# Two activations an octet in place of one over both layers, with the bias moved from TensorE into the activation, in a graph message kernel on one core

## The chip, the cores and the metric

One core of a Trainium2 chip. The metric is the device time of one execution in microseconds (us), the median of three runs, lower is better. The engines are named as in the profile: PE (TensorE matmuls), PEld (its weight loads), DVE (VectorE), ACT (ScalarE), POOL (GpSimd) and SP (SyncE, which here only issues DMAs).

## What is computed

```
x: 12500 x 64, src, dst: 400000 edges (dst sorted), edge_attr: 400000 x 16
m_in     = concat(x[src], x[dst], edge_attr)              # 144 wide
h        = silu(m_in @ W1 + b1)                           # 64 wide
messages = silu(h @ W2 + b2)
agg      = segment_sum(messages, dst)
out      = layernorm(x + silu(concat(x, agg) @ W3 + b3))
```

All of it is float32.

## The kernel before

The edges are cut into 3125 tiles of 128 edges, and eight tiles make an **octet**, so there are 391 octets; three octets make a chunk, for which destinations and attributes are loaded together. Because dst is sorted, an octet's edges fall in a window of 48 nodes. The first layer is split by its inputs. x W1a is a table in DRAM (`pa`), of which rows are gathered by source node. x W1b of the octet's 48 nodes, and W1c below it, stand in the weights `xw`, which multiply a one-hot matrix `oh` that has the attributes below it. Through the first 60 octets x W1b is computed by octet (`window_product`, `window_copy`); meanwhile `table_b` writes it for all nodes to a zero-padded DRAM table `pw1b`, 256 nodes at a time in octet steps 8 to 56, and from octet 60 (`OWN`) on SP fetches an octet's 48 rows from that table. In the kernel before, both ways add b1 on PE, by a matmul of a row of ones with `b1r` (lines 413 and 440).

The messages of an octet are summed on PE into `pg` by a second one-hot matrix `eh` (`add_up`, line 538), and DVE adds that to the window of the resident sums `agg` (`add_window`, line 543).

The source rows come in three ways. POOL gathers most with indirect DMAs of 128 rows (line 390). A tile pair of some octets (`pairs`) instead takes columns of the resident x, `xs`, copied one by one into a tile `cx` by ACT (`nc.scalar.copy`, line 317) and DVE (`tensor_reduce` over one element, line 315), with the column's address in a register that is loaded eight at a time (line 298), and PE multiplies them by W1a. A pair is 256 columns, so that every 256/144 = 1.78 octets one pair, two gathers, is taken from POOL. `ACOLS` and `VCOLS` say how many columns an octet step has on ACT and on DVE, each in two parts. A few pairs (`rpairs`) are fetched by SP row by row, 16 rows a step (line 341). The addresses of the columns are loaded by SP (line 368) into three rotating tiles `cxi` and scaled by DVE (line 376).

PE, ACT, DVE and SP run in the order written in the loop over octets, `for o in range(NO + 1)`. Within step o of the kernel before each engine has, in order:

- SP: index loads, `load` for the chunk that begins at o + 2, `window_load(o + 3)`, 16 rows.
- DVE: `add_window(o - 4)`, `compare_dst(o + 1)`, 40 columns, `window_copy(o + 1)` while o + 1 is below 60, `compare_nodes(o + 1)`, 32 columns, then addresses and node work.
- PE: `window_product(o + 1)`, `first_layer(o)`, `second_layer(o - 1)`, `table_b`, `add_up(o - 2)`, and in some steps a node product (lines 570 to 573).
- ACT: 72 columns, one Silu over 1024 elements a partition (line 524: the first layer of octet o and the second of o - 1, which share a two-bank PSUM tile `p12` and an output tile `hm`), the copy of `table_b`'s product (line 415) and its DMA to `pw1b` (line 416), and in some steps a node Silu (line 579).

Engines meet through semaphores. DMAs of SP and ACT share eight semaphores in rotation, and each of them waits until the DMA that had its semaphore before has completed.

Of the kernel before, what the change touches and what calls it, by code (L numbers as in the profile page):

```python
# [9 lines left out]
F32 = mybir.dt.float32  # L10
# [3 lines left out]
AF = mybir.ActivationFunctionType  # L14
OP = mybir.AluOpType
AX = mybir.AxisListType
PSUM = bass.MemoryType.PSUM
DRAM = bass.MemoryType.DRAM
ENG = mybir.EngineType

P = 128
G = 4
CT = 24
OT = 8
# [5 lines left out]
OWN = 60  # L30
XWB = 5
TABLES = 7
ACOLS = (40, 32)
VCOLS = (40, 32)
ROWS = 16
LOADS = 8
XBASE = (0, 64 << 18)
XADDR = 37344
LAG = CT * P // 32

U = 125
# [60 lines left out]
def windows(ctx, tc, ident, badi, pa, pw1b, x, xt, src_c, src_row, dst_c, dst_row, attr_t, dst_2, attr_2, base, w1, b1, w2, b2, w3, b3, out, edges):  # L102
    nc = tc.nc
    N, D = x.shape
# [3 lines left out]
    NO = base.shape[1]  # L108
    assert 2 * (S + A) == P and N + S <= NP
    E = 2 * S  # L110
    const = ctx.enter_context(tc.tile_pool(name="fconst", bufs=1))
# [16 lines left out]
    w1ab = const.tile([D, 2, D], F32, name="w1ab")  # L128
# [4 lines left out]
    nc.scalar.dma_start(left, b2.rearrange("(o k) -> o k", o=1))  # L133
    w1d = const.tile([P, P], F32, name="w1d")
    nc.vector.memset(w1d, 0.0)
    b1r = const.tile([1, 2, D], F32, name="b1r")
    nc.scalar.dma_start(b1r, b1.rearrange("(o s k) -> o s k", o=1, s=1).to_broadcast([1, 2, D]))
    w2d = const.tile([P, P], F32, name="w2d")
    nc.vector.memset(w2d, 0.0)
    w3s = const.tile([P, D], F32, name="w3s")  # L140
    for s in range(2):
        h = slice(s * D, (s + 1) * D)
        nc.scalar.dma_start(w1d[h, h], w1[0:D, :])
    XC = 2048
    xs = fast.tile([P, NP], F32, name="xs")

# [105 lines left out]
    octs = []  # L252
# [4 lines left out]
    with tc.tile_pool(name="gat", bufs=AHEAD + 2) as gat, tc.tile_pool(name="drp", bufs=2) as drp, \  # L257
            tc.tile_pool(name="hot", bufs=2) as hot, \
            tc.tile_pool(name="ehp", bufs=5) as ehp, \
            tc.tile_pool(name="work", bufs=2) as work, tc.tile_pool(name="win", bufs=3) as win, \  # L260
            tc.tile_pool(name="ps1", bufs=2, space=PSUM) as ps1, \
            tc.tile_pool(name="psa", bufs=1, space=PSUM) as psa, \
            tc.tile_pool(name="cx", bufs=4) as cx, tc.tile_pool(name="cxi", bufs=3) as cxi, \
            tc.tile_pool(name="rx", bufs=2) as rx, tc.tile_pool(name="rxi", bufs=2) as rxi, \
# [38 lines left out]
        def columns(o, eng, part):  # L303
            for j, e0, n in pieces(o, eng, part):
                regs = addresses(eng, j, e0, n)
                if pairs[j] not in cols:
                    cols[pairs[j]] = cx.tile([P, P], F32, name="cx")
                t = cols[pairs[j]].bitcast(U8)
                s = e0 // P
                h = slice(s * D, (s + 1) * D)  # L310
                for e, r in zip(range(e0 % P, e0 % P + n), regs):
                    to, frm = t[h, 4 * e:4 * e + 4], xb[h, ds(r - (XBASE[s] + XADDR), 4)]
                    if eng == ENG.DVE:

                        nc.vector.tensor_reduce(to, frm[:, :, None], AX.X, OP.max)  # L315
                    else:
                        nc.scalar.copy(to, frm)  # L317
# [53 lines left out]
        def address(o):  # L371
            for j in begun(o):
                t = indices[j]
                for s in range(2):
                    h = slice(s * P, (s + 1) * P)
                    nc.vector.tensor_scalar(t[:, h], t[:, h], 4.0, float(XBASE[s] + XADDR), op0=OP.mult, op1=OP.add)  # L376

# [26 lines left out]
        def table_b(c):  # L404

            n = min(2 * P, NP - c)
            k = (n + P - 1) // P
            ps = mis.tile([P, 2, D], F32, name="mm")
            t = pbs[c // (2 * P) % 2]
            for i in range(k):  # L410
                p = min(P, n - i * P)
                nc.tensor.matmul(ps[:p, i, :], xs[0:D, c + i * P:c + i * P + p], w1ab[:, 1, :], start=True, stop=False)
                nc.tensor.matmul(ps[:p, i, :], ones[:, :p], b1r[:, 0, :], start=False, stop=True)
            if n == 2 * P:
                nc.scalar.copy(t[:, :, D:], ps)
                nc.scalar.dma_start(pw1b[c:c + n, :].rearrange("(i p) d -> p i d", p=P), t)
                return
            for i in range(k):
                p = min(P, n - i * P)
                nc.scalar.copy(t[:p, i, D:], ps[:p, i, :])  # L420
                nc.scalar.dma_start(pw1b[c + i * P:c + i * P + p, :], t[:p, i, :])
# [14 lines left out]
        def window_product(o):  # L436
            pw = mis.tile([P, P], F32, name="mm")
            nc.tensor.matmul(pw[:E, :], winrow[o].rearrange("k s w -> k (s w)"), w1bb.rearrange("k s m -> k (s m)"),
                             start=True, stop=False)
            nc.tensor.matmul(pw[:E, :], ones[:, :E], b1r.rearrange("o s k -> o (s k)"), start=False, stop=True)  # L440
            winrow[o] = pw

        def window_copy(o):
# [10 lines left out]
                nc.sync.dma_start(dr[k * S:(k + 1) * S, e], dst_2[1 - k:2 - k, d].to_broadcast([S, e.stop - e.start]))  # L454
            nc.sync.dma_start(oh[E:, e], attr_2[:, d])

        hots, both, outs, messages, nodes_of = {}, {}, {}, {}, {}

        def compare_dst(o):
            c, t0, n, first, last = octs[o]  # L460
# [15 lines left out]
        def first_layer(o):  # L476
            c, t0, n, first, last = octs[o]
            n2 = n + n % 2
            k = n2 // 2
            ga = got.pop(o)  # L480
            oh, eh = hots.pop(o)
            both[o] = ps1.tile([P, 2, OT // 2, P], F32, name="p12")
            outs[o] = work.tile([P, 2, OT // 2, P], F32, name="hm")
            p1 = both[o][:, 0]
            nc.tensor.matmul(p1[:, :k], xw[o % XWB], oh, start=True, stop=False, skip_group_check=True)  # L485
            if o < RAW:
                pt = mis.tile([P, OT // 2, P], F32, name="mm")
                for i in range(k):
                    nc.tensor.matmul(pt[:, i, :], ga[:, 2 * i:2 * i + 2, :].rearrange("p s d -> p (s d)"), ident,
                                     start=True, stop=True)  # L490
                xg = outs[o][:, 0]
                nc.vector.tensor_copy(xg[:, :k], pt[:, :k])
                nc.tensor.matmul(p1[:, :k], w1d, xg[:, :k], start=False, stop=True, skip_group_check=True)
            if o in pairs:
                nc.tensor.matmul(p1[:, 0, :], w1d, cols.pop(o), start=False, stop=False, skip_group_check=True)  # L495
            for i in range(1 if o in pairs else 0, k if o >= RAW else 0):
                g2 = single.pop(o) if o in rpairs and i == 1 else ga[:, 2 * i:2 * i + 2, :]
                nc.tensor.matmul(p1[:, i, :], g2.rearrange("p s d -> p (s d)"), ident,  # L498
                                 start=False, stop=(i == k - 1), skip_group_check=True)
            nodes_of[o] = eh  # L500

        def second_layer(o):
            c, t0, n, first, last = octs[o]
            n2 = n + n % 2
            k = n2 // 2
            h = made.pop(o)
            if o + 1 == NO:
                both[NO] = ps1.tile([P, 2, OT // 2, P], F32, name="p12")
                outs[NO] = work.tile([P, 2, OT // 2, P], F32, name="hm")
            p2 = both[o + 1][:, 1].rearrange("p i (s d) -> p (i s) d", s=2)  # L510
            nc.tensor.matmul(p2[:, :n2, :], one3, b2r[:, :n2, :], start=True, stop=False, skip_group_check=True)  # L511
            for i in range(k):
                nc.tensor.matmul(p2[:, 2 * i:2 * i + 2, :].rearrange("p s d -> p (s d)"), h[:, i, :], w2d,  # L513
                                 start=False, stop=(i == k - 1), skip_group_check=True)

        def silus(o):

            pp = both.pop(o)
            hm = outs.pop(o)
            columns(o, ENG.Activation, 0)  # L520
            columns(o, ENG.Activation, 1)
            k = [-(-octs[q][2] // 2) if 0 <= q < NO else 0 for q in (o, o - 1)]
            if k == [OT // 2, OT // 2]:
                nc.scalar.activation(hm, pp, AF.Silu)  # L524
            else:
                for j in range(2):
                    if k[j]:
                        nc.scalar.activation(hm[:, j, :k[j]], pp[:, j, :k[j]], AF.Silu)
            made[o] = hm[:, 0]
            messages[o - 1] = hm[:, 1].rearrange("p i (s d) -> p (i s) d", s=2)  # L530

        def add_up(o):
            c, t0, n, first, last = octs[o]
            m, eh = messages.pop(o), nodes_of.pop(o)
            pg = sums[:, o % 4, :]
            for i in range(n):
                s = i % 2
                nc.tensor.matmul(pg[s * D:(s + 1) * D, :], m[:, i, :], eh[:, i, :],  # L538
                                 start=(i < 2), stop=(i >= n - 2), skip_group_check=True)
# [116 lines left out]
        with tc.manual_schedule(engines={ENG.PE, ENG.Activation, ENG.DVE, ENG.SP}):  # L656
            compare_dst(0)
            compare_nodes(0)
            for o in range(NO + 1):
# [59 lines left out]
                if o >= 1:  # L719
                    for c in tables[(o - 1) * per:o * per]:  # L720
                        table(c)
                if o >= 1:
                    second_layer(o - 1)
                silus(o)
                if 8 <= o < 8 + len(tables_b):
                    table_b(tables_b[o - 8])
                if o >= 2:
                    add_up(o - 2)
                address(o + 2)
                raddress(o + 2)  # L730
                rows(o)
# [295 lines left out]
```

## Time and profile before

| | us |
|---|---|
| median of 3 runs | 3783.2 |
| lowest, highest | 3776.93, 3786.62 |
| the profiled execution | 3786.62 |
| its span | 3784.8 |

| engine | busy us | share of the span |
|---|---|---|
| ACT | 3132.3 | 83% |
| DVE | 2711.0 | 72% |
| PE | 2674.0 | 71% |
| POOL | 2514.3 | 66% |

The profile is one execution, the highest of the three runs. Register loads, semaphore waits and DMA issues do not count as busy, so an engine that spends time on them can be full well below 100%. A group line gives an operation's line in the code, its engine, out<-in, shapes and count; then busy time and the mean length of one; then the idle time of the engine ahead of it and what ended that. "issue" means that nothing the profile shows ended it.

### The profile page before, as it was taken

How to read it: one execution, taken by the hardware profiler on the slowest of the kernel's cores; microseconds unless marked ns; L12 is line 12 of the kernel's file. 1: busy time of each engine (PE TensorE's matmuls, PEld its weight loads, DVE VectorE, ACT ScalarE, POOL GpSimd, SP SyncE). 2: the span in 40 equal slices, each digit the busy share in tenths (PEclk: the TensorE clock that was granted, in tenths of full speed). 3: DMA queues.
4: the chain of work that ended last, by engine and by line, in shares of the span. 5: the costliest groups of instructions: out<-in, count | busy, mean ns of one | idle time of the engine just before them, and what ended most of it. 6: DMA issues, size and time to landing. Idle time of an engine off the chain costs nothing. (4 is left out here: it accounts for less than half of the span.)

```text
span 3784.8 us, 115732 instructions
## 1 busy us (share of the span) xinstructions
PE 2674.0 (71%) x14985; PEld 1907.6 (50%) x14985; DVE 2711.0 (72%) x29094; ACT 3132.3 (83%) x27519; POOL 2514.3 (66%) x2666
## 2 busy tenths in 40 slices
PE   7988887766676676766666667666676666676666
PEld 5666565544454554544444444444454444454444
DVE  1376666777777777777777777777777777777775
ACT  2277777989889889898889898898898988988985
POOL 7665555667666667676676676676766666766763
PEclk9766667776767667777776767777667777666777
DMA  5532222223232232222323223223232232322322
GB/s 113 122 64 57 61 61 61 60 58 67 59 66 63 60 66 58 64 61 57 67 60 67 62 59 66 59 58 65 61 64 58 64 67 58 66 60 57 66 59 51
DMA packets 200383, 243.23 MB, mean 64 GB/s; under 512 B 86481, under 2 KB 139290, under 8 KB 198698
## 3 DMA queue, kind: packets, MB, share of 16 engines
q1 hardware_dynamic: 86360, 130.76, 15.0%
q0 software_dynamic: 85024, 87.23, 12.4%
q10 hardware_dynamic: 28210, 17.75, 1.9%
q14 instruction: 663, 5.43, 0.5%
q8 instruction: 126, 2.06, 0.2%
HBM read 222.64 MB, written 12.87 MB: 62 GB/s over the span
## 5 line engine op out<-in xcount | busy, mean ns | idle before, releaser
L390 POOL DMA_INDIRECT ga<-pa,sc x2561 | 2421.4, 945 | 1180.6 <-issue 672.7
L317 ACT COPY cx<-xs 64x4 uint8 x27016 | 2701.7, 188 | 169.0 <-issue 108.4
L315 DVE TENSOR_REDUCE cx<-xs 64x4 uint8 x27000 | 2062.7, 147 | 813.1 <-issue 764.8
L538 PE MATMUL pg<-eh,hm 128*64 128x48 f32 x6250 | 367.7, 280 | 899.1 <-DVE agg L543 898.7
L538 PEld LDWEIGHTS pg<-eh,hm 128*64 128x64 f32 x6250 | 309.2, 190 | 968.4 <-DVE agg L543 958.1
L485 PE MATMUL p<-oh,xw 128*128 128x512 f32 (+1 forms) x782 | 740.9, 1047 | 0.8 <-PE pg L538 0.5
L498 PEld LDWEIGHTS p<-ident,ga 128*128 128x128 f32 x2562 | 538.4, 296 | 153.2 <-issue 150.1
L513 PE MATMUL p<-w2d,hm 128*128 128x128 f32 x3126 | 519.9, 316 | 129.2 <-ACT hm L524 128.9
L513 PEld LDWEIGHTS p<-w2d,hm 128*128 128x128 f32 x3126 | 441.5, 218 | 259.6 <-ACT hm L524 150.8
L524 ACT ACTIVATE hm<-p 128x1024 f32<-128x1024 f32 x389 | 396.4, 1019 | 177.8 <-PE p L513 170.8
L498 PE MATMUL p<-ident,ga 128*128 128x128 f32 x2562 | 541.3, 377 | 0.0
L466 DVE TENSOR_TENSOR oh<-dr,wrow 96x512 f32<-96x512 int32 x391 | 263.0, 673 | 21.4 <-DMA dr<-in_dst 21.0
L495 PEld LDWEIGHTS p<-cx,w1d 128*128 128x128 f32 x422 | 135.2, 320 | 202.8 <-issue 202.8
L472 DVE TENSOR_TENSOR eh<-wrow,dc 128x384 f32<-128x384 f32 x391 | 213.9, 547 | 2.5
L485 PEld LDWEIGHTS p<-oh,xw 128*128 128x128 f32 x782 | 178.2, 283 | 39.9 <-issue 9.9
L511 PE MATMUL p<-b2r,one 3*128 3x512 bf16 x391 | 189.1, 484 | 0.0
L543 DVE TENSOR_TENSOR agg<-agg,pg 128x48 f32 x391 | 78.2, 200 | 130.2 <-PE pg L538 72.1
L579 ACT ACTIVATE z<-mm 128x256 f32<-128x256 f32 (+1 forms) x25 | 9.6, 383 | 195.6 <-PE mm L573 191.6
L495 PE MATMUL p<-cx,w1d 128*128 128x128 f32 x422 | 127.2, 403 | 0.0
L390 POOL DMA_INDIRECT ga<-in_x,sc x96 | 90.8, 946 | 34.8 <-issue 26.8
L376 DVE TENSOR_SCALAR cxi<-cxi 1x128 int32<-1x128 int32 x422 | 80.9, 244 | 1.6
L511 PEld LDWEIGHTS <-one 3*128 3x128 bf16 x391 | 36.9, 94 | 72.5 <-issue 52.5
(91 smaller groups left out, 911.0 us busy)
## 6 DMA issues: line engine op xcount, KB each, us to landing
rx<-pa SPq DMA_DIRECT2D x5888, 0.2 KB
dr<-in_dst SPq DMA_DIRECT2D x260, 288.0 KB
ga<-pa,sc POOLq DMA_INDIRECT x2561
oh<-in_attr SPq DMA_DIRECT2D x130, 192.0 KB
xw<-pw1b SPq DMA_DIRECT2D x331, 48.0 KB
pw1b<-pbs ACTq DMA_DIRECT2D x49, 128.0 KB
xs<-in_xt ACTq DMA_DIRECT2D x12, 512.0 KB
cxi<-in_src_row SPq DMA_DIRECT2D x211, 1.0 KB
```

The lines of the kernel that those rows point to most:

```text
L315: nc.vector.tensor_reduce(to, frm[:, :, None], AX.X, OP.max)
L317: nc.scalar.copy(to, frm)
L390: nc.gpsimd.indirect_dma_start(out=ga[:, i, :], out_offset=None, in_=x if o < RAW else pa[:, :], in_offset=bass.IndirectOffsetOnAxis(ap=sc ...
L466: nc.vector.tensor_tensor(oh[:E, :], dr[:, e:e + w], wn[:E, o:o + 1].to_broadcast([E, w]), op=OP.is_equal)
L472: nc.vector.tensor_tensor(eh[:, :n], row[:, None, :].to_broadcast([P, n, S]), rel[:, t0:t0 + n, None].to_broadcast([P, n, S]), op=OP.is_equal)
L485: nc.tensor.matmul(p1[:, :k], xw[o % XWB], oh, start=True, stop=False, skip_group_check=True)
L495: nc.tensor.matmul(p1[:, 0, :], w1d, cols.pop(o), start=False, stop=False, skip_group_check=True)
L498: nc.tensor.matmul(p1[:, i, :], g2.rearrange("p s d -> p (s d)"), ident, start=False, stop=(i == k - 1), skip_group_check=True)
L511: nc.tensor.matmul(p2[:, :n2, :], one3, b2r[:, :n2, :], start=True, stop=False, skip_group_check=True)
L513: nc.tensor.matmul(p2[:, 2 * i:2 * i + 2, :].rearrange("p s d -> p (s d)"), h[:, i, :], w2d, start=False, stop=(i == k - 1), skip_group_ch ...
L524: nc.scalar.activation(hm, pp, AF.Silu)
L538: nc.tensor.matmul(pg[s * D:(s + 1) * D, :], m[:, i, :], eh[:, i, :], start=(i < 2), stop=(i >= n - 2), skip_group_check=True)
```

## The change

The two halves are taken apart again. The first layer has a one-bank PSUM tile of its own, an activation of 512 elements a partition with b1 as its bias, and an output tile `h`; the second layer has the same in a pool `ps2`, with an output tile `m`, without bias. b1 is loaded as a 128x1 column `b1s`, and the matmuls that added b1 are gone from `table_b` and `window_product`. In a step `table_b` and `add_up(o - 2)` now stand ahead of `second_layer(o - 1)`, and ACT's columns are 32 before the first activation and 32 before the second, 64 in all where there were 72. DVE keeps its 72 columns, so a step has 136 columns and a pair is complete every 256/136 = 1.88 octets. `XADDR`, the address of `xs`, follows the changed layout.

```
-ACOLS = (40, 32)
+ACOLS = (32, 32)
 VCOLS = (40, 32)
...
-    b1r = const.tile([1, 2, D], F32, name="b1r")
+    b1s = const.tile([P, 1], F32, name="b1s")
...
+            tc.tile_pool(name="ps2", bufs=2, space=PSUM) as ps2, \
...
 def table_b(c):
-                nc.tensor.matmul(ps[:p, i, :], xs[0:D, c + i * P:c + i * P + p], w1ab[:, 1, :], start=True, stop=False)
-                nc.tensor.matmul(ps[:p, i, :], ones[:, :p], b1r[:, 0, :], start=False, stop=True)
+                nc.tensor.matmul(ps[:p, i, :], xs[0:D, c + i * P:c + i * P + p], w1ab[:, 1, :], start=True, stop=True)
...
 def window_product(o):
-                             start=True, stop=False)
-            nc.tensor.matmul(pw[:E, :], ones[:, :E], b1r.rearrange("o s k -> o (s k)"), start=False, stop=True)
+                             start=True, stop=True)
...
 def first_layer(o):
-            both[o] = ps1.tile([P, 2, OT // 2, P], F32, name="p12")
-            outs[o] = work.tile([P, 2, OT // 2, P], F32, name="hm")
-            p1 = both[o][:, 0]
+            p1 = ps1.tile([P, OT // 2, P], F32, name="p1")
...
+            columns(o, ENG.Activation, 0)
+            h = work.tile([P, OT // 2, P], F32, name="h")
+            nc.scalar.activation(h[:, :k], p1[:, :k], AF.Silu, bias=b1s)
...
 def second_layer(o):
-            p2 = both[o + 1][:, 1].rearrange("p i (s d) -> p (i s) d", s=2)
+            p2 = ps2.tile([P, OT, D], F32, name="p2")
...
+            columns(o + 1, ENG.Activation, 1)
+            m = work.tile([P, OT, D], F32, name="m")
+            nc.scalar.activation(m[:, :n2], p2[:, :n2], AF.Silu)
...
-        def silus(o):
-            columns(o, ENG.Activation, 0)
-            columns(o, ENG.Activation, 1)
-                nc.scalar.activation(hm, pp, AF.Silu)
...
 the loop, step o
-                if o >= 1:
-                    second_layer(o - 1)
-                silus(o)
                 if 8 <= o < 8 + len(tables_b):
                     table_b(tables_b[o - 8])
                 if o >= 2:
                     add_up(o - 2)
+                if o >= 1:
+                    second_layer(o - 1)
```

More of the change, by code (lines that the diff above doesn't have):

```diff
@@ L37 @@
 XBASE = (0, 64 << 18)
-XADDR = 37344
+XADDR = 36864
 LAG = CT * P // 32
@@ L135, in windows @@
     nc.vector.memset(w1d, 0.0)
-    b1r = const.tile([1, 2, D], F32, name="b1r")
-    nc.scalar.dma_start(b1r, b1.rearrange("(o s k) -> o s k", o=1, s=1).to_broadcast([1, 2, D]))
+    b1s = const.tile([P, 1], F32, name="b1s")
     w2d = const.tile([P, P], F32, name="w2d")
@@ L143, in windows @@
         nc.scalar.dma_start(w1d[h, h], w1[0:D, :])
+        nc.scalar.dma_start(b1s[h, :], b1.rearrange("(k o) -> k o", o=1))
     XC = 2048
@@ L455, in load @@
             nc.sync.dma_start(oh[E:, e], attr_2[:, d])
-        hots, both, outs, messages, nodes_of = {}, {}, {}, {}, {}
+        hots = {}
         def compare_dst(o):
@@ L490, in first_layer @@
                                      start=True, stop=True)
-                xg = outs[o][:, 0]
+                xg = work.tile([P, OT // 2, P], F32, name="m")
                 nc.vector.tensor_copy(xg[:, :k], pt[:, :k])
@@ L499, in first_layer @@
                                  start=False, stop=(i == k - 1), skip_group_check=True)
-            nodes_of[o] = eh
+            columns(o, ENG.Activation, 0)
+            h = work.tile([P, OT // 2, P], F32, name="h")
+            nc.scalar.activation(h[:, :k], p1[:, :k], AF.Silu, bias=b1s)
+            made[o] = h, eh
         def second_layer(o):
@@ L505, in second_layer @@
             k = n2 // 2
[L506 to L509, printed above, removed]
-            p2 = both[o + 1][:, 1].rearrange("p i (s d) -> p (i s) d", s=2)
+            h, eh = made.pop(o)
+            p2 = ps2.tile([P, OT, D], F32, name="p2")
             nc.tensor.matmul(p2[:, :n2, :], one3, b2r[:, :n2, :], start=True, stop=False, skip_group_check=True)
@@ L514, in second_layer @@
                                  start=False, stop=(i == k - 1), skip_group_check=True)
-        def silus(o):
-            pp = both.pop(o)
-            hm = outs.pop(o)
-            columns(o, ENG.Activation, 0)
-            columns(o, ENG.Activation, 1)
[L522 to L530, printed above, removed]
+            columns(o + 1, ENG.Activation, 1)
+            m = work.tile([P, OT, D], F32, name="m")
+            nc.scalar.activation(m[:, :n2], p2[:, :n2], AF.Silu)
+            made[o] = m, eh
         def add_up(o):
             c, t0, n, first, last = octs[o]
-            m, eh = messages.pop(o), nodes_of.pop(o)
+            m, eh = made.pop(o)
             pg = sums[:, o % 4, :]
```

## The prediction

> **What bounds the kernel now.** The chain of waits covers about 1% of the span and names nothing, so I went from the busy table to the idle time of single engines, stage by stage. The group lines of the page come first:
>
> ```profile
> L317 ACT COPY cx<-xs 64x4 uint8 x27016 | 2701.7, 188 | 169.0 <-issue 108.4
> L315 DVE TENSOR_REDUCE cx<-xs 64x4 uint8 x27000 | 2062.7, 147 | 813.1 <-issue 764.8
> L538 PE MATMUL pg<-eh,hm 128*64 128x48 f32 x6250 | 367.7, 280 | 899.1 <-DVE agg L543 898.7
> ```
>
> ACT is the busiest, yet PE waits 899 us for DVE, while the idle time of DVE is nearly all "issue". DVE's own waits between 700 and 3700 us say what that is:
>
> ```profile
> DVE cx L315 <- issue: 658.4, 2070, 0.8
> DVE agg L543 <- DVE cx L315: 7.1, 29, 0.4
> DVE agg L543 <- DVE cxi L376: 4.6, 26, 0.5
> ```
>
> There are 2070 gaps of 0.32 us, one between most groups of eight columns, where the registers are loaded. With 2274.7 us busy and 698 idle ahead of L315 these 3000 us of DVE are full; its waits for PE, ACT or a DMA sum to 3 us. So in this **late stage** DVE sets the pace: L543 starts at 703.5 us in step 60 and 3737.2 us in step 386, or 9.31 us an octet. POOL waits there 321.4 us for PE to free gather tiles (L498), and ACT, over the whole span, 171 us for PE ahead of L524 and 192 ahead of L579: neither is the bound.
>
> Before that the pace is 11.11 us (L543 at 171.7 us in step 12, 671.6 us in step 57). This **middle stage** is the one with `table_b`. ACT's timeline shows two of its steps:
>
> ```profile
> 411.81 0.24 ACT L415 COPY pbs<-mm 128x128 f32<-128x128 f32 x1
> 412.19 0.38 ACTq L416 DMA_DIRECT2D pw1b<-pbs  x1
> 413.22 7.25 ACT L317 COPY cx<-xs 64x4 uint8 x72 [1.17 <-issue]
> 420.49 1.02 ACT L524 ACTIVATE hm<-p 128x1024 f32<-128x1024 f32 x1
> 421.41 0.26 ACT L415 COPY pbs<-mm 128x128 f32<-128x128 f32 x1
> 425.87 0.38 ACTq L416 DMA_DIRECT2D pw1b<-pbs  x1
> 426.91 7.32 ACT L317 COPY cx<-xs 64x4 uint8 x72 [5.23 <-issue]
> ```
>
> ACT has no free time: after the copy L415 it stands until the table write L416 is issued, and the next columns follow 1.1 us after that. In the second step the write comes 4.2 us late. It waits for the semaphore of a row fetch of SP (L341). Over steps 12 to 56 these delays sum to 62 us, 1.4 an octet. ACT's sum is 7.37 (columns) + 1.02 + 0.25 + 1.06 + 1.4 = 11.1 us, the pace. SP is coupled back: it waits 96 us here (L368) for ACT's register loads, which free the index tiles.
>
> The **head**, to 171 us, is serial work of PE:
>
> ```profile
> 95.71 0.74 PE L438 MATMUL mm<-w1bb,xr 64*96 64x128 f32 x2
> 96.38 0.74 PE L440 MATMUL mm<-b1r,ones 1*96 1x128 f32 x2
> 97.05 2.08 PE L485 MATMUL p<-oh,xw 128*128 128x512 f32 x2
> ```
>
> Each bias product holds PE 0.67 us here, 0.38 where the clock is high.
>
> **The change, part by part.** Head: 11 of the 12 products L440 fall on PE's path (the first lies in a wait for a DMA), 7 at 0.67 and 4 at 0.38, 6.2 us; table_b in steps 8 to 11 loses two L413 each, at 0.36 to 0.61, about 3.5 us. PE's waits there for DVE (L493) stay. Head: -9 (-13 to -6).
>
> Middle: ACT's step loses 8 columns, 64/72 x 7.37 = 6.55, and gets two activations of 512 elements, which the 512-element row L528 gives at 0.594 each, for one of 1.02: +0.17. The bias operand has no row of this size; between nothing and 0.13 (L593 with a bias, 24 elements, 0.316, against 0.19 from the line through L528 and L524) I take none, the nearest row being L528. The columns now start twice a step, and starts inside a run show 0.15 to 0.3 us: +0.2. So 6.55 + 1.19 + 0.25 + 1.06 + 0.2 = 9.25 us without delays of the write. [...]
>
> The delay of the write is the open term. In the built order before, 13 of 45 writes follow, on their semaphore, a row fetch of the next octet step; these are 4.05 us late on average, the other 32 together about 10 us. After the change none follows the next step: 28 follow the same step, 16 the step before, one a write. But the write now stands ahead of the second run of columns and the second activation, some 4.2 us earlier in ACT's step. Lower bound: no delay, and DVE is the bound: 9.31, with window_copy 0.28 and limits and differences 0.25 (L717, L718, L230), less node work, 9.7 us. Upper: from 0.33 at a tie to the same step to 4.05 at one 9 us tighter, 4.2 us tighter gives 2.0, over 28 of 45 is 1.25: 10.5 us. SP's index load, released by ACT's last loads of the step before, reaches row nine 5.2 us later and lands at 7.2, one to two microseconds after the write is ready, in half the steps: I take 0.9, so 10.15 us. That gains 0.96 x 45 = 43 us (27 to 63). PE loses L440, two L413 and the wait of L412 for window_copy (22.8 us), but PE follows ACT here, so nothing more is counted. [...] The rows already show both clocks (L485 2.08 and 1.12 us); at the slow one PE's step without bias products is 1.0 + 0.7 + 1.9 + 1.9 + 0.5 + 1.6 + 1.2 = 8.8 us, still below 10.15.
>
> Late: DVE keeps 72 columns an octet. Twelve pairs fewer (199 for 211) take 24 of L376 at 0.17 and some 30 columns at 0.115 from it: -8 (-10 to -4). POOL gets 24 more gathers at 1.25 us, 30 us, under its 321 us of waits; without that cover they would cost 30. ACT's step falls from 8.2 to 7.7 us. The new queueing is PE's second_layer(o - 1) behind add_up(o - 2), which waits for DVE's L543 of the same step. From that L543 the message is ready after 0.2 + 1.1 (L538) + 1.9 (L511, L513) + 0.6 = 3.8 us; who waits is add_up(o - 1), 9.3 us later, and DVE only a step after that. Cover 5.5 us; if it were gone every microsecond over would cost 326. The node product now runs after second_layer, to about 6.7 us after L543, again inside 9.3; ACT's 190 us of waits for it (L579) mostly vanish, with no effect on DVE. DVE's group of eight takes 0.92 us whether or not ACT copies beside it, so a lighter ACT doesn't speed DVE.
>
> Tail: PE and ACT alternate for the last 40 us; the work is the same, 0 (+-3).
>
> Sum: -9 - 43 - 8 = -60 from the profiled 3786.6 (span 3784.8 and 1.8 around it): 3726.6. That execution was 3.4 above the median of its three, so **3723**.
>
> **Rivals.** (1) *The middle doesn't move:* the delays grow by what ACT saves, 1.8 us an octet. Then -17 is left: 3766. For it: ACT and SP wait for each other, and the upper bound of 2.0 is near if the 16 earlier ties stall too. Against: no tie to a next step is left. (2) *Slower, by the write:* SP isn't further ahead and the full shift of 4.2 us comes on top of 1.4 in each of 45 octets. ACT's step is 9.25 + 5.6 = 14.85, +3.75 x 45 = 169, less 17: 3935; at half the shift 3840. It decides once the mean delay passes 2.2 us (1.85 is even in the stage, the rest pays back head and late). (3) *ACT is the late bound after all*, as its 83% says: its step falls 0.4 to 0.5 us, x 326 is another -147: 3576. Against it stand DVE's 3 us of waits. (4) *The late stage slows because the message chain closes on DVE:* needs 5.5 us more an octet; nothing in the rows gives that.
>
> **How the numbers follow.** A measurement of this kernel can tell about 0.3%, 11.3 us, from no change. Forecast 72%: the ends of its terms give -86 and -37, so 3697 to 3746, and the spread of the runs before (3777 to 3787) widens that to 3690 to 3753. Rival 1 has 13%, over 3760 to 3785, rivals 2 and 4 together 11%, rival 3 4%. To leave out no more than 2 in 10 the range takes in rival 1: 3690 to 3781. Faster: 72 + 4 + 5 of rival 1, 81%; same 8%; slower 11%.
>
> **What would show it.** L440 and L413 with a bias gone; L543 from step 12 to 57 near 10.15 us apart on average, with 9.31 after step 60 unchanged and DVE's idle still "issue"; PE's wait at add_up still ended by DVE's L543 in the late stage; L579's wait gone; POOL's waits for L498 shorter by about 30 us. DVE waits for PE or ACT in the late stage, or writes L416 later than 2.2 us on average, would prove it wrong.

## The result and the profile after

The kernel after takes 3722.3 us (median of 4 runs, 3715.76 to 3726.66), the kernel before 3783.7 in the same comparison (4 runs, 3776.93 to 3786.62): a ratio of 0.9839, 95% interval 0.9818 to 0.986. The profiled execution after is 3726.66 us with a span of 3724.9. In the experiments further down every kernel, the one before included (5409 to 5519 us), ran at a slower pace; their ratios are taken against the kernel before on the same chip, and their stages, mostly of different chips, are compared only with each other.

The sum was -60 us and the span moved by -59.9, but not where it was put. By the starts of `add_window` (line 528 now), in one execution each, the slowest of the four on both sides:

| stretch | before, us | after, us | measured | predicted |
|---|---|---|---|---|
| head, to step 12 | 171.7 | 147.8 | -23.9 | -9 |
| middle, steps 12 to 57 | 499.9 (11.11 an octet) | 444.8 (9.88 an octet) | -55.1 | -43 |
| steps 57 to 60 | 31.9 | 28.0 | -3.9 | - |
| late, steps 60 to 386 | 3033.7 (9.31) | 3061.3 (9.39) | +27.6 | -8 |
| tail | 47.6 | 43.1 | -4.6 | 0 |

The groups of the page that stood first in the prediction are now these:

```profile
L316 DVE TENSOR_REDUCE cx<-xs 64x4 uint8 x26944 | 2058.4, 148 | 813.8 <-issue 764.3
L318 ACT COPY cx<-xs 64x4 uint8 x24000 | 2403.6, 188 | 133.8 <-issue 102.2
L523 PE MATMUL pg<-eh,m 128*64 128x48 f32 x6250 | 357.2, 273 | 1047.3 <-DVE agg L528 996.7
L514 ACT ACTIVATE m<-p 128x512 f32<-128x512 f32 x391 | 232.9, 596 | 443.1 <-PE p L510 427.4
L499 ACT ACTIVATE h<-p,b1s 128x512 f32<-128x512 f32 x391 | 267.1, 683 | 54.9 <-PE p L490 41.5
```

ACT has lost 3000 copies and waits more (443 us ahead of L514), PE waits more for DVE, and DVE's columns and their "issue" time are what they were. So DVE bounds the late stage as before. The two activations differ only in the bias operand: 683 against 596 ns.

DVE's waits in the late stage (engine and line, what it waited for: us in total, times, longest) hold one line that was not there:

```profile
DVE cx L316 <- issue: 670.8, 2111, 0.7
DVE agg L528 <- PE mm L558: 21.9, 19, 1.8
DVE agg L528 <- DVE cx L316: 9.8, 37, 0.6
```

L558 is the node product, which reads `agg`, while L528 writes it. The timeline shows what happens (start, us, operation, idle time before it and what ended it), first PE's, then two rows of DVE's:

```profile
1011.18 1.10 PE L523 MATMUL pg<-eh,m 128*64 128x48 f32 x16 [3.82 <-DVE agg L528]
1012.21 0.60 PE L508 MATMUL p<-b2r,one 3*128 3x512 bf16 x1
1012.74 2.08 PE L510 MATMUL p<-w2d,h 128*128 128x128 f32 x8
1014.75 1.22 PE L555 MATMUL mm<-b3r,ones 1*128 1x256 f32 x2
...
1020.49 0.73 PE L558 MATMUL mm<-w3s,agg 128*128 128x64 f32 x2
```

```profile
1010.83 0.20 DVE L528 TENSOR_TENSOR agg<-agg,pg 128x48 f32 x1 [0.57 <-DVE cx L316]
...
1021.25 0.20 DVE L528 TENSOR_TENSOR agg<-agg,pg 128x48 f32 x1 [1.34 <-PE mm L558]
```

`second_layer` (L508, L510) takes 2.5 us between `add_up` and the node product. The product then ends 10.4 us after the add_window ahead of it, and DVE's next add_window, due after 9.1, stands for 1.34 us. The loss lies in these steps: the 20 intervals from one add_window to the next that hold a node product went from 9.00 to 10.14 us on average, 22.8 us together, the other 306 from 9.33 to 9.34.

The middle, on ACT's timeline, answers to the two steps shown of before:

```profile
398.68 0.68 ACT L499 ACTIVATE h<-p,b1s 128x512 f32<-128x512 f32 x1
399.26 0.25 ACT L415 COPY pbs<-mm 128x128 f32<-128x128 f32 x1
399.54 0.38 ACTq L416 DMA_DIRECT2D pw1b<-pbs  x1
400.57 3.32 ACT L318 COPY cx<-xs 64x4 uint8 x32 [1.06 <-issue]
403.91 0.60 ACT L514 ACTIVATE m<-p 128x512 f32<-128x512 f32 x1
404.53 3.09 ACT L318 COPY cx<-xs 64x4 uint8 x32
407.65 0.69 ACT L499 ACTIVATE h<-p,b1s 128x512 f32<-128x512 f32 x1
408.24 0.26 ACT L415 COPY pbs<-mm 128x128 f32<-128x128 f32 x1
411.07 0.38 ACTq L416 DMA_DIRECT2D pw1b<-pbs  x1
```

ACT's step is 9 us where the write goes out at once (399.54), and 2.5 us longer where the write waits (411.07). From the end of the copy to the write, the 45 writes of the stage now lose 29.9 us; the same count gives 66.7 before. One of them is over 3 us late, where 12 were; in all 13 cases what ended the wait is a row fetch of SP (`rx`).

The head, on PE's timeline, has no product L440 any more; the first layer follows the window product directly:

```profile
97.21 0.74 PE L438 MATMUL mm<-w1bb,xr 64*96 64x128 f32 x2
97.88 2.08 PE L482 MATMUL p<-oh,xw 128*128 128x512 f32 x2
...
120.89 0.46 PE L438 MATMUL mm<-w1bb,xr 64*96 64x128 f32 x2
121.28 1.13 PE L482 MATMUL p<-oh,xw 128*128 128x512 f32 x2
```

### The profile page after: what moved, and what is told of

The parts are those of the page before. It is cut to its first block, busy times and chain, and to the rows that moved or that the text cites. A ratio compares the mean times of both kernels' runs of the same rounds, so it can differ in the third digit from the quotient of the medians.

```text
span 3724.9 us, 112677 instructions
## 1 busy us (share of the span) xinstructions
PE 2581.7 (69%) x14667; PEld 1910.2 (51%) x14667; DVE 2703.3 (73%) x29014; ACT 2912.8 (78%) x24892; POOL 2535.2 (68%) x2690
## 5 line engine op out<-in xcount | busy, mean ns | idle before, releaser
L318 ACT COPY cx<-xs 64x4 uint8 x24000 | 2403.6, 188 | 133.8 <-issue 102.2
L523 PE MATMUL pg<-eh,m 128*64 128x48 f32 x6250 | 357.2, 273 | 1047.3 <-DVE agg L528 996.7
L523 PEld LDWEIGHTS pg<-eh,m 128*64 128x64 f32 x6250 | 309.0, 184 | 1108.1 <-issue 630.5
L510 PE MATMUL p<-w2d,h 128*128 128x128 f32 x3126 | 743.6, 413 | 0.0
L510 PEld LDWEIGHTS p<-w2d,h 128*128 128x128 f32 x3126 | 633.9, 301 | 143.5 <-issue 143.5
L482 PE MATMUL p<-oh,xw 128*128 128x512 f32 (+1 forms) x782 | 672.8, 959 | 27.8 <-DVE xw L443 27.6
L514 ACT ACTIVATE m<-p 128x512 f32<-128x512 f32 x391 | 232.9, 596 | 443.1 <-PE p L510 427.4
L495 PEld LDWEIGHTS p<-ident,ga 128*128 128x128 f32 x2586 | 448.5, 248 | 160.5 <-issue 147.2
L495 PE MATMUL p<-ident,ga 128*128 128x128 f32 x2586 | 439.4, 321 | 0.0
L499 ACT ACTIVATE h<-p,b1s 128x512 f32<-128x512 f32 x391 | 267.1, 683 | 54.9 <-PE p L490 41.5
L508 PE MATMUL p<-b2r,one 3*128 3x512 bf16 x391 | 207.1, 530 | 0.0
L528 DVE TENSOR_TENSOR agg<-agg,pg 128x48 f32 x391 | 78.0, 200 | 102.6 <-PE pg L523 46.3
L564 ACT ACTIVATE z<-mm 128x256 f32<-128x256 f32 (+1 forms) x25 | 9.6, 383 | 125.5 <-PE mm L558 125.5
```

The source lines that it names most:

```text
L499: nc.scalar.activation(h[:, :k], p1[:, :k], AF.Silu, bias=b1s)
L514: nc.scalar.activation(m[:, :n2], p2[:, :n2], AF.Silu)
```

## The experiments

Theory, formed on the two profiles: the late stage pays for the node product behind `second_layer`; the middle gains by ACT's shorter step and by the write's delays; the head gains twice, by the bias products themselves and by shorter durations of PE's other products. The rivals: the head's level is chance, the middle gains by the columns alone or by the write alone, the late loss has another cause.

**The change itself at the later pace.** The kernel after and the kernel before, each once more:

> The kernel after, unchanged, as the base for the runs of its variants and as a second look at the head. If this run is at the pace of the first profiles (about 3720 us): theory of the clock in the head, step 12 again at 145 to 152 us because the removed bias products let PE reach its higher clock earlier; rival, the head is a matter of chance: step 12 anywhere from 147 to 165 us. If it is at the pace of the runs that took about 5400 us: the change is worth less there, since DVE and ACT stand for something other than their work; from the variants (0.995 with the node product first, 0.997 with the bias on PE) I expect 0.996 to 1.000 of the kernel before. At either pace the node product ends 10.4 us after the add_window ahead of it, the last 20 times of the late stage, where it was 7.7 us before.

> The kernel before, unchanged, for the split into stages at the pace of the later runs. Theory: the change acts by stage as in the first pair of profiles: PE's busy time up to step 12 is 150 to 157 us here, against 124 to 131 in three profiles of the order after without the bias products, and step 12 comes at 227 to 240 us against 216 to 221; in the late stage no add_window waits for a node product, which ends 7.7 us after the add_window ahead of it; in the middle at least ten writes of table_b come over 3 us late, against one in each profile of the kernel after. Rival: the differences of the first pair are those of single executions: PE's busy time up to step 12 at 125 to 145, late writes no more than three.

Measured: after 0.9961 of before (0.9935 to 0.9987); the kernel before against itself 1.0002 (0.9978 to 1.0025). By stage, before and after: step 12 at 241.5 and 216.2 us, middle 674.8 and 687.2, late 4513.7 and 4520.1. So only the head's gain is there at this pace. The node product ends 7.76 and 10.38 us (medians of 20) after the add_window ahead of it, as in the first pair; ten writes of `table_b` are over 3 us late before, one after, but of the ten only three end with a row fetch and seven with "issue". PE's busy time to step 12 is 161.8 us before, above the 150 to 157 that I expected, and 131.0 after. Against my expectation four add_windows of the kernel before wait for the node product here, 6.5 us in all. So the head, the end of the node product and the count of late writes differ in a second pair as in the first; the gain of the middle doesn't come back.

**The node product ahead of `second_layer`.**

```
                 if o >= 2:
                     add_up(o - 2)
+                for f, a in todo.get(o, []) if o < NO else []:
+                    if f is node_product:
+                        f(*a)
                 if o >= 1:
                     second_layer(o - 1)
```

> The kernel after, with the node product of a step issued on PE between add_up(o - 2) and second_layer(o - 1) instead of behind second_layer; nothing else moves. Theory: the late stage lost 27.5 us (9.306 to 9.390 us an octet) because DVE's add_window of the next step must wait until the node product has read the sums, and that product now stands behind second_layer; DVE's 19 waits for it (21.9 us) shrink below 3 us, steps 60 to 386 take 3035 to 3042 us, the whole about 3700 us. Rival: the late stage is slower for another reason (more address conversions, the bias pointer, the halves of ACT's columns) and the waits only show up in its place: 3718 to 3726 us.

> The kernel after, with the node product of a step issued on PE between add_up(o - 2) and second_layer(o - 1) instead of behind second_layer; nothing else moves. (On the first chip that this kernel ran on, every kernel took about 5500 us; this run is to be read at the pace of the first profiles.) Theory: the late stage lost 27.5 us (9.306 to 9.390 us an octet) because DVE's add_window of the next step must wait until the node product has read the sums, and that product now stands behind second_layer; DVE's 19 waits for it (21.9 us) shrink below 3 us, steps 60 to 386 take 3035 to 3042 us, the whole about 3700 us. Rival: the late stage is slower for another reason (the bias pointer, the halves of ACT's columns) and the waits only show up in its place: 3718 to 3726 us.

Measured on two chips: 0.9958 (0.9932 to 0.9985) and 0.9949 (0.992 to 0.9979) of before; the kernel after had 0.9961. The time can't decide: 22 us are 0.4% here, and the late stage of this one kernel took 4469 us on one chip and 4395 on the other. The wait can. DVE's waits in the late stage, first of the kernel after at this pace, then of this one:

```profile
DVE agg L528 <- issue: 98.6, 74, 6.3
DVE agg L528 <- PE mm L558: 19.0, 11, 2.3
```

```profile
DVE agg L528 <- issue: 108.1, 78, 4.8
...
DVE agg L528 <- PE mm L558: 2.5, 1, 2.5
```

On the second chip the line is missing altogether. The product ends 7.85 us after the add_window in both profiles, where it ended at 10.38. So the order of these two steps on PE makes most of the wait, and moving the product takes it down to what the kernel before has at this pace (6.5 us). That 22 us of time come back with it was not measured; that they are lost in the 20 node steps, the intervals of the first pair show.

**`second_layer` back in its old place.**

```
+                if o >= 1:
+                    second_layer(o - 1)
                 if 8 <= o < 8 + len(tables_b):
                     table_b(tables_b[o - 8])
                 if o >= 2:
                     add_up(o - 2)
-                if o >= 1:
-                    second_layer(o - 1)
```

> The kernel after, with second_layer(o - 1) back where it was, ahead of table_b and add_up(o - 2) on PE; ACT's second columns and second Silu then also come ahead of the copy of table_b. Theory of the node product: it again follows add_up directly, so the late stage falls as in the run with the node product first, to 3035 to 3042 us, the whole 3700 us, plus or minus 10 for the middle, where ACT's table copy and its write move to the end of the step. Rival: if second_layer behind add_up costs by itself (the message chain), this one gains more than the one with the node product first, by 10 us or more in the late stage.

Measured: 1.0202 (1.0166 to 1.0237), slower than both kernels. The product ends at 7.85 us again and no add_window waits for it, as the theory has it; but the late stage takes 4588.6 us, the longest of all. Neither theory has that, and what makes it slower stays open.

**Bias products back on PE.** `b1r` and the matmuls of lines 413 and 440 as before, the first activation without bias, the rest as after.

```
-            nc.scalar.activation(h[:, :k], p1[:, :k], AF.Silu, bias=b1s)
+            nc.scalar.activation(h[:, :k], p1[:, :k], AF.Silu)
```

> The kernel after, with b1 added on PE again by the matmuls of table_b and window_product, and the first activation without a bias operand. Theory: in the head the bias products cost their own 9 us and lower the clock level of the serial PE work besides, so step 12 comes 15 to 24 us later than 147.8; the middle moves by -4 (the bias pointer's 87 ns, 45 times) to 0; the late stage stays at 3055 to 3065 us. The whole 3733 to 3745. Rival: the head's level is a matter of chance from one execution to the next and not of the change: about +9 in the head, 3727 to 3732. Second rival: the bias operand is what slowed the late stage: late at 3035, the whole 3705 to 3715.

> The kernel after, with b1 added on PE again by the matmuls of table_b and window_product, and the first activation without a bias operand. Theory: in the head the bias products cost their own 9 us and lower the clock level of the serial PE work besides, so step 12 comes 15 to 24 us later than 147.8; the middle moves by -4 (the bias pointer's 87 ns, 45 times) to 0; the late stage stays at 3055 to 3065 us. The whole 3733 to 3745. Rival: the head's level is a matter of chance from one execution to the next and not of the change: about +9 in the head, 3727 to 3732. Second rival: the bias operand is what slowed the late stage: late at 3035, the whole 3705 to 3715.

Measured: 0.9984 (0.9959 to 1.0009) and 0.9966 (0.9946 to 0.9987). Step 12 comes at 238.3 and 226.7 us, where the kernel after has 216.2. PE's busy time to there is 157.4 and 149.5 against 131.0, so 18 to 26 us more for bias products that take 11 to 12. The late stage, 4495 and 4440, is inside the spread of its neighbours, and still waits for the node product (23.3 us, 14 times, on the second chip): the bias operand doesn't make these waits. Whether it has a part in the few us that are left, a spread of this size hides. A miss: the middle is 661.7 and 654.9 us, 12 to 44 us shorter than the 673 to 699 of the three profiles with the order of after. PE's wait for ACT's table copy falls there from 143 to 270 us to 74 and 81. Five and seven writes are over 3 us late in these two shorter middles, where the kernel after has one, so at this pace late writes alone don't set the middle's length. What does, these runs don't say.

**The kernel before without the bias products.**

```
-  ... w1ab[:, 1, :], start=True, stop=False)
-  nc.tensor.matmul(ps[:p, i, :], ones[:, :p], b1r[:, 0, :], start=False, stop=True)
+  ... w1ab[:, 1, :], start=True, stop=True)
```

and the same in `window_product`.

> The kernel before without the matmuls that add b1 in table_b and window_product; b1 is left out of the first layer altogether, nothing else changes. Theory for the head: the bias products cost more than their own 9 to 11 us, because the other products of PE run at longer durations beside them; PE's busy time up to step 12 falls by 20 to 28 us, from 139.8 at the first profiles' pace (from 149 to 157 at the pace of the later runs), and step 12 comes 20 to 25 us earlier at the first pace, 10 to 20 at the later one. Rival: only the products' own time goes, 9 to 12 us of PE's busy time. Middle: PE follows ACT there, so nothing of the middle's gain comes from these products: at the first pace steps 12 to 57 stay within 10 us of 499.9; rival: PE's lighter step shortens the write's delays or window_copy's waits and 20 us or more go. Whole at the first pace 3755 to 3765 us, at the later one 0.993 to 0.999 of the kernel before.

Measured: 0.9983 (0.996 to 1.0005), step 12 at 230.9 us, PE's busy time to there 149.9. Against the kernel before (161.8, and 156.1 in the run with 64 columns, whose head is the same) that is 6 to 12 us: the rival, the products' own time. So my theory of the head was too simple. The runs together make a table of four cells, PE's busy time to step 12 in us, one value a profile; 140.6 is the run with `second_layer` back, the rest of the upper row has the kernel before, with its one activation:

| | b1 on PE | no b1 on PE |
|---|---|---|
| order of before (`second_layer` ahead of `table_b`) | 161.8, 156.1 | 149.9, 140.6 |
| order of after | 157.4, 149.5 | 131.0, 124.5, 127.0, 125.7, 132.2, 134.9 |

The first pair has 139.8 top left and 115.1 bottom right. In the kernel before, taking the products out alone is worth 9 us (149.9 against a mean of 159.0). The rest of the change with the products kept is worth 6 (153.5), and all of it 30 (129.2), twice the two together. The order alone, in the kernel after, is worth 11 (140.6 against 129.2), on one profile; single profiles of a cell differ by up to 11. What exceeds the products' own 11 to 12 us is in products that didn't change, such as `table`'s (line 185), here of the kernel before without bias products and then of the kernel after:

```profile
119.35 7.09 PE L185 MATMUL mm<-w1ab,xs 64*128 64x64 f32 x32
137.25 7.09 PE L185 MATMUL mm<-w1ab,xs 64*128 64x64 f32 x32
```

```profile
118.18 3.78 PE L185 MATMUL mm<-w1ab,xs 64*128 64x64 f32 x32
131.28 3.78 PE L185 MATMUL mm<-w1ab,xs 64*128 64x64 f32 x32
```

The same 32 products take 3.78 or 7.09 us, and some runs of them lie between. The clock that PE was granted in just these stretches, as a share of full speed, is the third figure from the end, first of the kernel before without bias products, then of the kernel after:

```profile
119.35:126.40 7.05, 7.05 (x34) 6.93 (x33) 0.00 (x0) 0.59 (x1) 5.53 (x6) 0.50 0.32 65
137.25:144.30 7.05, 7.05 (x34) 6.93 (x33) 0.00 (x0) 0.59 (x1) 5.53 (x6) 0.50 0.69 135
```

```profile
118.20:121.90 3.70, 3.70 (x35) 3.63 (x34) 0.00 (x0) 1.27 (x2) 2.79 (x4) 0.99 0.19 34
131.30:135.00 3.70, 3.70 (x35) 3.63 (x34) 0.00 (x0) 1.27 (x2) 2.78 (x4) 1.00 1.03 231
```

So the long duration is that at half the clock, 0.50, and the short one that at 1.00. Only with the new order and without bias products do more of them fall on the short side: all products of this kind, `table_b`'s among them, take 30.7 to 34.2 us to step 12 in the seven profiles of that cell (31.1 in the first pair), and 34.9 to 42.6 in the other three cells.

**ACT's columns.** 72 in the kernel after, and 64 in the kernel before:

```
-ACOLS = (32, 32)
+ACOLS = (40, 32)
```

> The kernel after, with ACT's columns back at 40 and 32 an octet. Theory: in the middle stage ACT's sum sets the pace, 8 columns are 0.8 us, so steps 12 to 57 go from 444.8 to about 480 us (9.88 to 10.67 an octet); in the late stage DVE sets the pace and ACT has room, so 3061 us moves by no more than 10. The whole: 3750 to 3768 us. Rival: the middle's gain came from the earlier table write and its semaphore, not from the columns: middle within 10 us of 444.8, the whole 3722 to 3735.

```
-ACOLS = (40, 32)
+ACOLS = (32, 32)
```

> The kernel before, with ACT's columns cut to 32 and 32 and nothing else. Theory: the 8 columns are 0.82 us of ACT's step, and ACT's sum sets the middle stage's pace, so steps 12 to 57 fall from 499.9 to 455 to 465 us (11.11 to about 10.25 an octet) if the write's delays stay at 1.4 us an octet; the late stage stays near 3026 to 3034; the whole 3735 to 3745 us. Rival: the delays of the write grow by what ACT saves, since the write waits for row fetches of SP that keep their own pace: middle 495 to 500, the whole 3775 to 3784.

Measured: 1.005 (1.0033 to 1.0066) and 1.0078 (1.0053 to 1.0103), both slower than before. The middle takes 684.6 us with 72 columns in the kernel after, inside the 673 to 699 of its three profiles with 64; and 658.4 with 64 in the kernel before, 16 less than its 674.8 on another chip. Neither shows the 35 us that 8 columns should be worth. At this pace ACT stands for "issue" 257 us (72 columns, after) and 176 us (64, before) in the middle beside its work, so these two runs don't tell what the columns are worth at the first pace; they are inconclusive. With 72 columns the late stage has 46.9 us of waits for the node product (16 times); why the kernel before gets slower as a whole with 64, no profile shows.

**The table write on POOL's queue.**

```
-                nc.scalar.dma_start(pw1b[c:c + n, :].rearrange("(i p) d -> p i d", p=P), t)
+                nc.gpsimd.dma_start(pw1b[c:c + n, :].rearrange("(i p) d -> p i d", p=P), t)
```

> The kernel after, with table_b's write to pw1b issued by POOL instead of ACT. ACT then never waits for the semaphore of a row fetch of SP, nor spends the 1.06 us from the copy to the next columns. Theory of the middle (ACT's sum with the write's delay is the pace): at the pace of the first profiles 0.66 us of delay and up to 1 us of issue an octet go, until DVE's floor of 9.3 to 9.7 is met, so steps 12 to 57 fall from 444.8 to 420 to 436 us; at the pace of the later runs from about 687 (673 to 699 in three profiles) by 30 to 70. Rival: the delay only fills time that ACT would spend waiting for PE's products or for SP anyway, or POOL's write waits for the copy and delays its gathers instead: steps 12 to 57 within 20 us of 687, or longer. The whole 0.985 to 0.994 of the kernel before by the theory, 0.995 to 1.000 by the rival.

Measured: 0.9869 (0.9824 to 0.9915), and the middle takes 619.8 us, 54 to 79 less than the three profiles with the write on ACT, as the theory said. ACT's timeline shows the step without the write: the columns follow the copy at once.

```profile
522.25 0.68 ACT L499 ACTIVATE h<-p,b1s 128x512 f32<-128x512 f32 x1
522.83 0.25 ACT L415 COPY pbs<-mm 128x128 f32<-128x128 f32 x1
522.98 3.15 ACT L318 COPY cx<-xs 64x4 uint8 x32
```

POOL pays: it stands 58.3 us for the copy, and its waits for PE (L495) shrink from 298.2 to 131.9 us. So the write on ACT is on the path of the middle, also where the columns no longer show.

**DVE with 64 columns, the node product first.**

```
-VCOLS = (40, 32)
+VCOLS = (32, 32)
```

> The kernel after with the node product first, and DVE's columns cut to 32 and 32 as well (128 columns an octet in all, a pair every two octets). Theory: DVE sets the late pace; a group of eight is 0.92 us, so the pace falls from 9.31 to about 8.5 us, until POOL is met: 8 - 2/2 - 2/16 = 6.875 gathers of 1.25 us are 8.6 us. Late 2800 to 2880 us, middle 415 to 440, the whole 3440 to 3560 us. Rival: POOL's gathers cost more when they are not waiting for PE, or SP's 16 row fetches set the pace: late 2950 to 3050, the whole 3600 to 3700 us.

Measured: 0.9786 (0.9754 to 0.9818), the fastest of all kernels that ran and 1.8% below the kernel after's ratio. The late stage takes 4341.2 us against 4395.3 on the same chip with 72 columns: 54 us, where 8 columns at 0.92 us over 326 octets would be 300. At this pace DVE's columns are on the path, but not alone: its add_window alone stands 311.8 us there until something that the profile calls "remote" (another core or an unknown queue), and 90.1 us for the node product (13 times), although that is in its earlier place. It beats both kernels here; its time at the first pace was not measured.

## Why the prediction held, and where it didn't

The total held by luck: the terms were off by -15 (head), -12 (middle) and +36 us (late), and -8.5 us in stretches put at nothing (steps 57 to 60 and the tail) closed the sum.

**Head, -9 predicted, -23.9 measured: mis-sized.** The step "11 of the 12 products L440 fall on PE's path ... 6.2 us; table_b ... about 3.5" priced the products that go, and kept the duration of all others. Their own time is 10.9 us in the first profile, near the 9.7 of the step. The other 14 us are unchanged products at shorter durations: PE's busy time to step 12 fell by 24.7 us, of which `table` and `table_b` without bias 3.8, `first_layer`'s L490 3.8, the transposes L486 3.8. The rows of before already showed both durations (2.08 and 1.12 us) and the prediction cited them, but only to bound a slow step. They are those at the two granted clocks, in the kernel before 0.50 at 97.05 us and 1.00 at 125.55: from 115.3 us to the end of the head the kernel after has 1.00 throughout, the kernel before changes between 0.50 and 1.00. The table of four cells shows that most of it takes more than one part of the change. What decides the clock was not settled.

**Middle, -43 predicted, -55.1 measured: right in kind.** Per octet, ACT's columns went from 7.30 to 6.43 us (-0.87, predicted -0.82), the activations from 0.95 to 1.20 (+0.25, predicted +0.17), and the time ahead of the columns, in which the write lies, from 2.56 to 1.83. The last is the term that was off: -0.73, where the prediction had the delay fall from 1.4 to 0.9 and added 0.2 for restarts, so -0.3. The restarts cost next to nothing (in the timeline above the columns start at 404.53 us, 0.02 after the activation's end), and the delay fell to 0.66 where the prediction's 1.4 is 1.48 by the same count. DVE is now close behind ACT: 334.2 us busy and 87.3 of "issue" are 421.5 of the 444.8. That the write on ACT, its wait and its issue together, is on the path, the POOL run shows at its own pace; the share of the columns it doesn't, and no run at the first pace does. So the split of the -55.1 is a sum of ACT's rows, not the result of an experiment.

On the bias operand the prediction was wrong. I took nothing for it, by the row without bias. The row with it is 683 ns against 596, so 87 ns, 45 times, 4 us of the middle, inside the 0 to 0.13 us that the prediction had set as its limits.

**Late, -8 predicted, +27.6 measured: wrong, by a step of the text.** "The node product now runs after second_layer, to about 6.7 us after L543, again inside 9.3" is the step. It left the product about 3.5 us (6.7 less 0.2, 1.1 and 1.9), where 15 of the 20 late products of the kernel before take 6.47, at a granted clock of 0.50, and none under 5.9. The product ended at 7.73 us already before and ends at 10.38 now: in the timeline above 0.35 us to `add_up`, 1.03 for it, 2.54 for `second_layer` and 6.47 for the product itself (1014.75 to 1021.22). Its next customer is DVE's add_window, 9.3 us on, so 19 of 20 node steps wait, 1.15 us on average, 21.9 us. The prediction had named "DVE waits for PE or ACT in the late stage" as what would prove it wrong; it did, for this stage. The other 6 us are spread: 5.9 us of waits for ACT ahead of DVE's columns where there were 1.5, and 2.7 more behind its own columns. And the 8 us for fewer address conversions never came: DVE's busy time went from 2300.7 to 2299.9 us.

**Tail and cover.** The tail lost 4.6 us, just outside the 3 allowed. POOL's waits for PE fell from 443.3 to 370.2 us, where 30 were expected; nearly all of it in the middle (113.8 to 43.7), none in the late stage (323.1 to 324.4). ACT's wait for the node product did not vanish: 125.5 us after 191.6, since the product itself comes later.

**The rivals.** Rivals 1 to 3 were not met: the middle moved, the write's delays fell, and a lighter ACT didn't speed the late stage. Rival 4, a slower late stage because a chain through PE closes on DVE, was set aside with "needs 5.5 us more an octet; nothing in the rows gives that". Its kind is what happened, by the node product instead of the messages and in 20 octets instead of 326.

## What to carry to other kernels

When a step is moved in an engine's order, time every later step of that engine from the event that starts it to its last reader, the rare ones too, with the durations that the rows show: a step that runs in every sixteenth octet cost 22 of the 55 us that the middle won. A total that comes out right proves nothing of its terms; take the stages apart before believing any of them. A DMA issued by the engine that sets the pace can be worth moving to a queue with slack, for its issue and its wait for a semaphore: in the kernel after ACT's next columns start 1.03 us after the write's issue (399.54 and 400.57 us), and the 45 writes lost 29.9 us by waiting; moving them to POOL's queue took 54 to 79 us off about 687, in one profile at the slower pace.

## What the runs showed of the hardware

The same 32 products of PE take 3.78 us at a granted clock of 1.00 and 7.09 at 0.50, and both durations stand in one profile (the kernel before at the pace of the experiments, 3.78 at 109.65 us and 7.09 at 122.13). Which of them is common changed with two edits that touch other products: all products of this kind take 30.7 to 34.2 us to step 12 with both edits, 34.9 to 42.6 otherwise. Steady work didn't raise the clock in one profile: in the kernel before without bias products PE is busy 38.4 of the 40 us from 110 to 150 us, has no gap over 0.85 us there, and the clock is 0.50 throughout. Up to its first record of the clock, at 73.5 us, the profile of the kernel before shows 1.00, and yet L485 takes 2.08 us at 51.79, as it does at 0.50 later (97.05).

At the pace of the experiments the instruction streams of PE, ACT, DVE and SP slow down together. DVE's timeline of the kernel after:

```profile
2005.76 0.15 DVE L316 TENSOR_REDUCE cx<-xs 64x4 uint8 x1 [1.27 <-issue]
2006.47 0.15 DVE L316 TENSOR_REDUCE cx<-xs 64x4 uint8 x1 [0.56 <-issue]
2007.20 0.15 DVE L316 TENSOR_REDUCE cx<-xs 64x4 uint8 x1 [0.57 <-issue]
```

Single columns come 0.71 us apart, at an unchanged duration, in stretches of 4 to 5 us about every 13 us; of 265 such stretches on ACT between 1000 and 4500 us, 231 overlap one on DVE. In these stretches of ACT, a third of the time, ACT starts 1.4 instructions of all kinds a us, against 7.6 outside; DVE 2.3 against 8.6, SP 1.6 against 3.6, PE 1.7 against 3.1. POOL, with 0.6 in both, doesn't slow down. Every kernel took 47 to 50 ns of span for each instruction of its record (5506.4 us for 112677 after), where the first pair took 33. What holds the streams back, no run here shows.
